# Scan layer: depthwise convolutions in a queue of their own, one per step, interleaved with the other background items

## The chip, the cores and the metric

The kernel runs on one core of one Trainium2 chip. The metric is the device time of one execution in microseconds (us); several executions are taken, and their median counts.

The core's engines run side by side and each takes its own instructions in order: TensorE (PE in the profile; PEld is its loading of weights), VectorE (DVE), ScalarE (ACT), GpSimd (POOL), and SyncE (SP), which here only issues transfers.

## The reference, cut to what matters

The program is four layers on an image batch `x` of shape (8, 64, 64, 64). Only the first one, a selective scan, is touched. For each image, with L = 64 x 64 = 4096 places, DI = 128 channels, N = 16 states and K = 4 directions (rows, columns, and both backwards):

```
xz   = layernorm(x) @ in_proj_w.T + in_proj_b          # 64 -> 2 x 128
xi,z = split(xz)
u    = silu(depthwise_conv_3x3(xi) + conv_b)           # 9 taps
for each direction k (u read in that order):
    dt, B, C = softplus(...), ..., ...                 # projections of u
    h[n,t] = h[n,t-1] * exp(dt[t] * A[n]) + dt[t] * B[n,t] * u[t]      # n = 0..15
    y     += sum_n h[n,t] * C[n,t]  + D * u
y    = layernorm(y) * silu(z)
x    = x + y @ outproj_w.T + outproj_b
```

After that come the second half of layer 0 (a small convolution block), two attention layers and a channel-mixing layer with a few steps of gradient descent.

## The kernel before, in words

`scan_layer` puts the 128 channels on the partitions. An image is worked in 16 **steps**: four directions (`k`, in the order 0, 2, 1, 3, where 1 and 3 are the column orders; for the last image 1, 3, 0, 2) by four chunks (`c`) of CH = 1024 places. A step has 16 **turns**, one for each state `n`. There are eight images (`b`), so 2048 turns, written in one long program order inside `tc.manual_schedule()`: each engine gets its instructions in the order in which the Python code issues them.

The main work of turn n, in the order of the code:

- `empty` (L692): on ScalarE, copies a finished sum of a step from PSUM into `y`.
- `spread` for turn n+1: brings B of that state on all partitions. In twelve of the sixteen turns PE does it with two bf16 products (`z`, L646). In the turns of `BY_POOL` = (0, 3, 6, 8) it is done by a broadcast transfer (`bt`, L624), a product on POOL (`product`, L636, three turns ahead) and a copy by ScalarE to PSUM (L643).
- `sum_up` (L719): PE adds the product `ct` of an earlier turn (two or three turns back, `LAG` = 2) to the sum `yps` in PSUM, as two f32 products of 512 columns with the identity. Turn 3 (`LAG + 1`) has no `sum_up`, but `begin_sum` (L710), which starts the sum of this step from `y` or from `u`; turn 7 (`LAG + 5`) has two `sum_up`.
- a slot for one **background item** (`bg.before`), see below.
- `load` (L624): a broadcast transfer of C of turn n+1 into `ct`, on SP's queue.
- `decay` (L628) for turn n+2: exp on ScalarE.
- `save_state` (L664) and `product` (L636).
- `unit`: on DVE a product (L673, not in the turns of `BY_POOL`) and the scan itself (L677); on POOL the product with C (L682).
- `bg.after`: the second half of the background item that was started one turn earlier.

The step's end feeds the next step: `hooks` issue, in fixed turns, the softplus of the next step's `dt` (L546, L549, L552) and the splitting of B into bf16 pieces (L581 to L608).

**Background items** are pairs (`make`, `use`): `make` issues the products on PE into a PSUM buffer, `use` the copy or activation that empties it, one turn later. All items of a kind take their PSUM buffer from one tag, `mm`, which has two buffers of 512 f32 columns; `z` has two of 1024, `yps` one of 1024. The class `Background` holds one queue: each turn's slot pops one item. A skipped slot leaves it alone: the slot of turn 7 always, that of turn 4 in column orders. The items are, in the order in which an image's items stand in the queue:

- for the next step, put at the front: two `lower` (PE L514 `dps`, ScalarE L522 `e`), two `step_size` (PE L532 `tps`, ScalarE L540 and L541), and in column orders first a copy of `u` in column order on ScalarE (L558, `turn`);
- `after`, for the image before: the norm of `y` (PE L296 and L309, ScalarE L300 to L316, transfers, L329 and L332, then PE L346 with DVE L350 and ScalarE L351), and the output projection of eight blocks (PE L470 and L471 `ops`, ScalarE L477, with POOL L464 for the gating product `z` times `y`, and loads `xr` and `z` on SP);
- `before`, for the image after: loads of `x` (`xn`), its norm (the same lines), the projection into the padded image `pad` (PE L383 `xps`, ScalarE L389), eight gates (PE L399 `zps`, ScalarE L406, a Silu, and a store `zd`), and eight convolutions, one per block of 512 places. A convolution is nine products on PE (L421 `vps`, one per tap) into one PSUM buffer, cut into parts; its last part is followed by a Silu on ScalarE (L430) into `u`.

Items (None, None) are spacers: they take a slot and issue nothing. A new image is entered in the queue at step 1 (`start`), the finished one at step 0. At the last step of each image `bg.drain()` issues whatever still waits; half of the next image's convolutions are then entered again (`rest`), except for the last image, all of whose convolutions are in the queue from the start.

Of the kernel before, what the change touches and what calls it, by code (L numbers as in the profile page):

```python
# [18 lines left out]
NB = 8  # L19
# [4 lines left out]
NBK = L // BK  # L24
DI = 128
N = 16
R = 4
CH = 1024
NCH = L // CH
# [136 lines left out]
class Background:  # L166
# [2 lines left out]

    def __init__(self):
        self.queue, self.last, self.late = deque(), None, []

    def add(self, items, first=False):
        if first:
            self.queue.extendleft(reversed(items))
        else:
            self.queue.extend(items)

    def later(self, do):
        self.late.append(do)

    def before(self, skip=False):
        self.now = None
        if self.queue and not skip:
            make, use = self.queue.popleft()
            self.now = (use, make() if make else None)

    def after(self):  # L190
# [7 lines left out]
    def surplus(self, turns):  # L198

        return max(0, -((turns - len(self.queue)) // (turns + 1)))  # L200

    def drain(self):
        while self.queue or self.last or self.late:
            self.before()
            self.after()


def scan_layer(cm, x_in, w, xh):

    tc, nc = cm.tc, cm.nc  # L210
    with ExitStack() as ctx:
# [156 lines left out]
        def before(b):  # L368
# [42 lines left out]
            def convolve(j):  # L411

                held = []

                def part(t0, t1):
                    def make():
                        if t0 == 0:
                            held.append(bank("vps"))
                        for t in range(t0, t1):
                            dy, dx = divmod(t, 3)  # L420
                            nc.tensor.matmul(  # L421
                                held[0].rearrange("p (r c) -> p r c", c=S), convd[:, t, :],
                                pad[:, j * rows + dy : (j + 1) * rows + dy, dx : dx + S],
                                start=(t == 0), stop=(t == 8),
                            )

                    return make

                def use(_):
                    nc.scalar.activation(u[:, bass.ts(j, BK)], held[0], AF.Silu, bias=convb)  # L430

                if b == 0:
                    return [(part(0, 5), None), (part(5, 9), use)]
                if b == NB - 1:
                    return [
                        (part(0, 3), None), (part(3, 5), None), (part(5, 7), None),
                        (part(7, 9), use),
                    ]
                return [
                    (part(0, 2), None), (part(2, 4), None), (None, None), (part(4, 6), None),  # L440
                    (part(6, 8), None), (None, None), (part(8, 9), use),
                ]

            items = [[(None, load(j)) for j in range(NBK)]]
            for blocks in (FIRST if b == 0 else (range(NBK),)):
# [4 lines left out]
        def after(b, y, zd, blocks=range(NBK)):  # L450
# [39 lines left out]
            items = norm_items(y, DI, lno, on_g, on_b, blocks)  # L490
            items.insert(-2, (None, lambda _: [load(j) for j in blocks[:3]]))
            items += [(None, begin), (None, None)]
            out = [[project_out(j), (None, None)] for j in blocks]
            return items + sum(out, [])[:-1]

        def ordered(t, k, c):

# [242 lines left out]
        def prepare(b, s):  # L740

            if b not in images:
                return None
            u, zd, y = images[b]
            k, c, i = steps(b)[s]
            dt, bc, ut, e, items, soft = project(u, k, c)
            if b == 0 and s < NCH:
                items = later.pop(s, []) + items + [(None, soft[0]), (None, soft[1])]
            bg.add(items, first=True)
            new = work.tile([DI, N], F32, name="state", tag="state", bufs=3)  # L750
            ctl = dict(
                k=k, c=c, u=u, y=y, dt=dt, bc=bc, ut=ut, dus=e, soft=soft, new=new, state=None,
                first=(i == 0), new_y=(s < NCH), turns=(s % (2 * NCH) == NCH - 1),
            )
            ctl["pieces"] = pieces(ctl)
            return ctl

        later, rest = {}, {}  # L760

        def start(b):
            u, zd, items, gates, convs = before(b)
# [6 lines left out]
                    later[s] = sum(items[s + 1 : s + 2], []) + convs[2 * s] + convs[2 * s + 1]  # L770
                later[NCH] = gates
            else:
                bg.add(gates)
                now = NBK // 2 if b < NB - 1 else NBK
                for conv in convs[:now]:
                    bg.add(conv)
                rest[b] = convs[now:]


        with tc.manual_schedule():  # L780
# [15 lines left out]
            for b in range(NB):  # L796
                for s in range(4 * NCH):
# [3 lines left out]
                    if s + 1 < 4 * NCH:  # L801
                        nxt = prepare(b, s + 1)
                    else:
                        bg.drain()
                        nxt = prepare(b + 1, 0)
                        bg.add(sum(rest.pop(b + 1, []), []))
                    hooks = {}
                    if nxt:
                        do = nxt["pieces"]
# [18 lines left out]
                    for n in range(N):  # L828
                        empty()
                        ahead(spread, n + 1)  # L830
                        if n == LAG + 1:
                            bg.before()
                            begin_sum()
                        else:
                            twice = n == LAG + 5
                            if len(pending) > LAG:
                                sum_up()
                            if twice:
                                sum_up()
                            skip = twice or (n == LAG + 2 and ctl["k"] % 2 == 1)  # L840
                            bg.before(skip and not early and not late)
                        if (n + 5) % N in BY_POOL and not (early and n + 5 == N):
                            ahead(load, n + 5, 0)
                        ahead(load, n + 1, 1)
# [1181 lines left out]
```

## Time and profile before

| what | value |
|---|---|
| time, median of 3 runs | 12565.19 us (12553.39 to 12569.26) |
| the profiled execution: its own time | 12567.77 us |
| its span, first to last instruction | 12566.0 us |
| scan layer, first to last scan | 98.2 to 7257.4 us |
| widths of images 0 to 7 | 955.2, 883.8, 880.7, 877.6, 879.3, 878.2, 903.4, 901.2 us |
| scan on DVE, L677, mean of one | 2341 ns, or 2282 ns for the first chunk of a direction |
| product with C on POOL, L682, mean of one | 2359 ns |
| product on DVE, L673, mean of one | 1215 ns |
| granted TensorE clock, mean | 0.956 |

The profile page gives the busy time of each engine over the span, a strip of 40 slices, the chain that ended last, and the costliest groups of instructions with what ended the idle time before them. The windows view gives the same busy times for any stretch; the timeline gives single instructions with, in brackets, the idle time of their engine just before them and what ended it. Widths of steps are the distance between the scans (L677) that begin them; there are 16 scans to a step. The steps of images 1 to 5 repeat each other to within a microsecond or two.

### The profile page before, as it was taken

What the parts mean: (1) busy time and instruction counts of PE and PEld (TensorE: products, weight loads), DVE (VectorE), ACT (ScalarE), POOL (GpSimd) and SP (SyncE); (2) the same over time, 40 slices, a digit from 0 to 9 for tenths busy, and PEclk for the clock granted to TensorE, in tenths of its full rate; (3) what the DMA queues carried; (4) which work ended last, traced back from release to release, by engine and by line L of the source; (5) the groups of instructions that cost most, each with busy time, mean ns of one, the idle gap of its engine ahead of it and who ended that gap; (6) DMA issues with size and microseconds to landing.
All of it is one profiled execution on the core that took longest, in us unless ns stands there. A gap on an engine that the chain in (4) does not pass through costs nothing. (4 is left out here: it accounts for less than half of the span.)

```text
span 12566.0 us, 122564 instructions
## 1 busy us (share of the span) xinstructions
PE 11561.6 (92%) x39403; PEld 4098.9 (33%) x39403; DVE 10385.0 (83%) x7362; ACT 7996.2 (64%) x10740; POOL 7424.1 (59%) x3638
## 2 busy tenths in 40 slices
PE   7899999999999999999998889999987778999999
PEld 2233233233232332332332222332324463333333
DVE  4999999999989999999899858768687685676767
ACT  4777677777776776777776536546456584555554
POOL 4999999999999999999899810000004490000000
PEclk8999999999999999999999989999998788999999
DMA  3666666666656656656566510000011110000000
GB/s 96 211 203 205 213 203 204 213 201 211 211 197 220 204 196 220 205 200 219 191 200 211 186 47 15 17 24 6 18 38 39 40 25 23 12 11 17 6 11 6
DMA packets 547044, 1562.30 MB, mean 124 GB/s; under 512 B 133040, under 2 KB 150096, under 8 KB 543824
## 3 DMA queue, kind: packets, MB, share of 16 engines
q1 hardware_dynamic: 546384, 1554.33, 37.6%
q8 instruction: 314, 5.14, 0.2%
q14 instruction: 346, 2.83, 0.1%
HBM read 1456.35 MB, written 88.87 MB: 123 GB/s over the span
## 5 line engine op out<-in xcount | busy, mean ns | idle before, releaser
L682 POOL TENSOR_TENSOR ct<-ct,h 128x1024 f32<-128x1024 f32 x2048 | 4796.0, 2359 | 456.2 <-DVE h L677 197.7
L719 PE MATMUL yps<-ct,ident 128*128 128x512 f32 x8192 | 4071.2, 626 | 4.6 <-POOL ct L682 4.6
L677 DVE TENSOR_TENSOR_SCAN h<-a,state,z 128x1024 f32<-128x1024 f32 x1536 | 3572.2, 2341 | 102.7 <-POOL ct L682 30.8
L1027 DVE TENSOR_TENSOR sum<-sum,ex 128x1024 f32<-128x1024 f32 x1920 | 2348.1, 1223 | 617.9 <-ACT ex L1020 481.2
L1020 ACT ACTIVATE ex<-sc 128x1024 f32<-128x1024 f32 x2048 | 1967.9, 1024 | 1359.8 <-PE sc L1015 1359.8
L628 ACT ACTIVATE a<-dt,amat 128x1024 f32<-128x1024 f32 x2048 | 2344.7, 1146 | 611.5 <-DVE h L677 606.9
L673 DVE TENSOR_TENSOR z<-z,e 128x1024 f32<-128x1024 f32 x1536 | 1866.5, 1215 | 391.1 <-PE z L646 240.2
L719 PEld LDWEIGHTS yps<-ct,ident 128*128 128x128 f32 x8192 | 1444.8, 192 | 2033.2 <-issue 1816.6
L1034 PE MATMUL av<-ex,v 128*64 128x512 f32 x8192 | 1950.0, 604 | 0.0
L1015 PE MATMUL sc<-q,k 16*128 16x512 f32 (+1 forms) x8192 | 1562.2, 623 | 4.2 <-ACT q L1008 3.1
L677 DVE TENSOR_TENSOR_SCAN h<-a,z 128x1024 f32<-128x1024 f32 x512 | 1162.7, 2282 | 101.6 <-ACT z L643 85.9
L646 PE MATMUL z<-bs,pick 48*128 48x512 bf16 x3072 | 941.6, 387 | 324.7 <-DVE h L677 290.0
L636 POOL TENSOR_TENSOR bt<-bt,e 128x1024 f32<-128x1024 f32 x512 | 1209.1, 2362 | 4.7 <-DMA bt<-bc 4.7
L1341 POOL TENSOR_TENSOR gt<-gt,pad 128x1024 f32<-128x1024 f32 x16 | 34.9, 2179 | 1572.0 <-ACT gt L1340 1492.7
L1034 PEld LDWEIGHTS av<-ex,v 128*64 128x64 f32 x8192 | 512.2, 136 | 1332.8 <-issue 1278.9
L1015 PEld LDWEIGHTS sc<-q,k 16*128 16x128 f32 (+1 forms) x8192 | 528.4, 184 | 1016.2 <-issue 977.3
L643 ACT COPY z<-bt 128x1024 f32<-128x1024 f32 x512 | 519.4, 1014 | 460.4 <-DVE h L677 237.7
L646 PEld LDWEIGHTS <-pick 48*128 48x128 bf16 x3072 | 180.1, 95 | 1592.7 <-issue 756.6
L421 PE MATMUL vps<-pad,convd 128*128 128x512 f32 x1152 | 540.6, 594 | 0.0
L1714 DVE RECIPROCAL r<-e 128x512 f32<-128x512 f32 x128 | 420.7, 3324 | 0.0
L1717 POOL TENSOR_TENSOR r<-r,half 128x512 f32<-128x512 f32 x128 | 162.6, 1270 | 361.6 <-issue 188.8
L664 ACT COPY state<-h 128x1 f32<-128x1 f32 x2048 | 359.4, 176 | 1.6 <-DVE h L677 1.6
(408 smaller groups left out, 10581.9 us busy)
## 6 DMA issues: line engine op xcount, KB each, us to landing
ct<-bc SPq DMA_DIRECT2D x2048, 512.0 KB
bt<-bc SPq DMA_DIRECT2D x512, 512.0 KB
x<-x SPq DMA_DIRECT2D x12, 2048.0 KB
bc<-e SPq DMA_DIRECT2D x256, 64.0 KB
zd<-z SPq DMA_DIRECT2D x64, 256.0 KB
z<-zd SPq DMA_DIRECT2D x64, 256.0 KB
x<-x SPq DMA_DIRECT2D x32, 512.0 KB
part<-x SPq DMA_DIRECT2D x128, 128.0 KB
```

The lines of the kernel that those rows point to most:

```text
L421: nc.tensor.matmul(held[0].rearrange("p (r c) -> p r c", c=S), convd[:, t, :], pad[:, j * rows + dy : (j + 1) * rows + dy, dx : dx + S], s ...
L628: ctl["exp", n] = nc.scalar.activation(ctl["a", n], ctl["dt"], AF.Exp, scale=amat[:, ctl["k"], n : n + 1])
L636: nc.gpsimd.tensor_tensor(bt, bt, ctl["dus"], ALU.mult)
L646: nc.tensor.matmul(z[:, bass.ts(i, BK)], pick[:, n : n + 1].to_broadcast([3 * N, DI]), ctl["bs"][:, bass.ts(i, BK)], start=True, stop=True,)
L673: first = nc.vector.tensor_tensor(z, z, ctl["dus"], ALU.mult)
L677: nc.vector.tensor_tensor_scan(h[:, flip], a[:, flip], z[:, flip], 0.0 if state is None else state[:, n : n + 1], ALU.mult, ALU.add,)
L682: freed[at] = nc.gpsimd.tensor_tensor(ct, ct, h, ALU.mult)
L719: nc.tensor.matmul(ctl["ps"][:, bass.ts(i, BK)], cm.ident, ct[:, bass.ts(i, BK)], start=False, stop=(n == N - 1 and not ctl["turns"]),)
L1015: nc.tensor.matmul(sc[:, e, :], k[r : r + d, bass.ts(j, 128)], qs[i][r : r + d, :], start=True, stop=True,)
L1020: nc.scalar.activation(ex, sc, AF.Exp)
L1027: nc.vector.tensor_tensor(sums[i], sums[i], ex, ALU.add)
L1034: nc.tensor.matmul(avs[i][r, :], v[:, j, r], ex[:, e, :], start=(j == 0), stop=(j == TQ - 1))
```

## The change

The convolutions get a queue of their own (`groups`), one group of parts for each convolution. A group is opened only when all its parts fit in the slots that are left in the current step, and when nothing that was put at the front for the next step still waits. While a group is open, its parts alternate with items of the ordinary queue (`item` says that the last slot went to one), unless as many parts are left as slots. `credit` allows one group per step, two in the steps of image 6. The groups become available when the image's last projection has been issued. `finish` issues what is still missing when a step is about to read `u`; it takes the place of the drain at the last step of an image. In column orders the skipped slots are those of turns 3 and 7, except in the first step of the second direction of the pair, which skips turn 7 alone. The spacers inside a convolution and between the output projections go; each gate is followed by two spacers instead.

```diff
 class Background:
     def __init__(self):
         self.queue, self.last, self.late = deque(), None, []
+        self.groups, self.open, self.done = deque(), deque(), {}
+        self.first = self.credit = 0
+        self.item = False
     def add(self, items, first=False):
         if first:
             self.queue.extendleft(reversed(items))
+            self.first += len(items)
...
-    def before(self, skip=False):
+    def before(self, skip=False, slots=0):
         self.now = None
-        if self.queue and not skip:
-            make, use = self.queue.popleft()
+        if skip:
+            return
+        src = None
+        if self.open:
+            if not self.first and (self.item or len(self.open) >= slots or not self.queue):
+                src = self.open
+        elif self.groups and self.credit and not self.first and slots >= len(self.groups[0]):
+            src = self.open = self.groups.popleft()
+            self.credit -= 1
+        if src is None and self.queue:
+            src = self.queue
+            self.first = max(0, self.first - 1)
+        self.item = src is not self.open
+        if src:
+            make, use = src.popleft()
             self.now = (use, make() if make else None)
...
+    def finish(self, b, count):
+        while self.done.get(b, NBK) < count:
+            self.credit = 1
+            self.before(slots=NBK)
+            self.after()
...
                 def use(_):
                     nc.scalar.activation(u[:, bass.ts(j, BK)], held[0], AF.Silu, bias=convb)
-                if b == 0:
-                    return [(part(0, 5), None), (part(5, 9), use)]
-                if b == NB - 1:
-                    return [
-                        (part(0, 3), None), (part(3, 5), None), (part(5, 7), None),
-                        (part(7, 9), use),
-                    ]
-                return [
-                    (part(0, 2), None), (part(2, 4), None), (None, None), (part(4, 6), None),
-                    (part(6, 8), None), (None, None), (part(8, 9), use),
-                ]
+                    if b:
+                        bg.done[b] += 1
+                cuts = (0, 5, 9) if b == 0 else (0, 3, 5, 7, 9) if b == NB - 1 else (0, 2, 4, 6, 8, 9)
+                parts = [(part(t0, t1), None) for t0, t1 in zip(cuts, cuts[1:])]
+                return parts[:-1] + [(parts[-1][0], use)]
...
-            out = [[project_out(j), (None, None)] for j in blocks]
-            return items + sum(out, [])[:-1]
+            return items + [project_out(j) for j in blocks]
...
             k, c, i = steps(b)[s]
+            bg.finish(b, 2 * c + 2 if s < NCH and k == 0 else NBK)
...
             else:
-                bg.add(gates)
-                now = NBK // 2 if b < NB - 1 else NBK
-                for conv in convs[:now]:
-                    bg.add(conv)
-                rest[b] = convs[now:]
+                bg.done[b] = 0
+                bg.add([(None, lambda _: bg.groups.extend(deque(conv) for conv in convs))])
+                for gate in gates:
+                    bg.add([gate, (None, None), (None, None)])
...
                     else:
-                        bg.drain()
                         nxt = prepare(b + 1, 0)
-                        bg.add(sum(rest.pop(b + 1, []), []))
+                    bg.credit = 2 if b == NB - 2 else 1
+                    columns = ctl["k"] % 2 == 1 and s % (2 * NCH) != NCH
+                    idle = () if early or late else (LAG + 1, LAG + 5) if columns else (LAG + 5,)
...
+                        slots = 0 if early or late else sum(m not in idle for m in range(n, N))
                         if n == LAG + 1:
-                            bg.before()
+                            bg.before(n in idle, slots)
                             begin_sum()
                         else:
-                            twice = n == LAG + 5
                             if len(pending) > LAG:
                                 sum_up()
-                            if twice:
+                            if n == LAG + 5:
                                 sum_up()
-                            skip = twice or (n == LAG + 2 and ctl["k"] % 2 == 1)
-                            bg.before(skip and not early and not late)
+                            bg.before(n in idle, slots)
```

More of the change, by code (lines that the diff above doesn't have):

```diff
@@ L200, in surplus @@
         return max(0, -((turns - len(self.queue)) // (turns + 1)))
+    def finish(self, b, count):
[3 more added lines that the diff above has]
+            self.after()
     def drain(self):
-        while self.queue or self.last or self.late:
+        while self.queue or self.open or self.last or self.late:
             self.before()
@@ L756, in prepare @@
             return ctl
-        later, rest = {}, {}
+        later = {}
         def start(b):
```

## The prediction

> **Notation.** Step s (0 to 15) is one of an image's 16 (direction, chunk) pairs, turn n (0 to 15) one state inside it; images are 0 to 7. Turn lengths are read in the timeline as the distance between two scans (L677).
>
> **What bounds the kernel now.** I read the page's first part, then the table of windows cut at image and step borders, then the timeline of the turns that were long.
>
> ```profile
> PE 11561.6 (92%) x39403; PEld 4098.9 (33%) x39403; DVE 10385.0 (83%) x7362; ACT 7996.2 (64%) x10740; POOL 7424.1 (59%) x3638
> ```
>
> These are means over four layers; only the first, from 98.2 to 7257.4 us, is touched. The windows of images 0, 3 and 6, then of steps 3, 12 and 14 of image 3 (columns: PE, PEld, DVE, ACT, POOL busy, clock, DMA share, GB/s):
>
> ```profile
> 98.20:1053.36 955.16, 859.11 (x1914) 284.58 (x1915) 821.25 (x464) 663.73 (x940) 826.25 (x383) 0.95 0.57 188
> 2817.78:3695.35 877.57, 833.77 (x1897) 273.21 (x1896) 822.02 (x467) 637.59 (x923) 839.46 (x393) 0.98 0.63 208
> 5452.81:6356.18 903.37, 857.73 (x1945) 282.22 (x1943) 822.75 (x467) 648.28 (x932) 839.04 (x393) 0.98 0.61 202
> ...
> 2982.05:3033.90 51.85, 46.78 (x110) 14.83 (x108) 51.42 (x32) 36.37 (x54) 51.85 (x25) 1.00 0.64 215
> ...
> 3467.90:3527.07 59.17, 53.20 (x118) 18.40 (x117) 50.63 (x29) 45.32 (x61) 48.85 (x23) 0.91 0.61 200
> ...
> 3582.99:3638.53 55.54, 53.53 (x124) 18.91 (x123) 51.00 (x30) 38.48 (x54) 52.24 (x25) 0.97 0.56 197
> ```
>
> POOL is the wall. Step 3 is POOL from end to end (51.85 of 51.85). Image 3 keeps POOL busy 839.46 of 877.57 us, so 38 us are idle; DVE, at 822, is just behind. POOL's floor for a plain step is (839.46 - 8 x 1.26 of gating products, L464) / 16 = 51.8 us; DVE's is 12 turns of 3.50 and 4 of 2.26, 51.0 us. What can be won is POOL's idle time, and it lies where convolutions and gates are: step 12 idles 59.17 - 48.85 = 10.3 us. Two causes show in the timeline.
>
> (a) The run of eight gates. ScalarE, POOL and DVE around the start of step 12:
>
> ```profile
> 3464.90 1.28 ACT L406 ACT_TABLE_LOAD   x1
> 3466.20 0.69 ACT L406 ACTIVATE z<-zps,inb 128x512 f32<-128x512 f32 x1
> 3466.78 1.02 ACT L643 COPY z<-bt 128x1024 f32<-128x1024 f32 x1
> 3467.82 1.28 ACT L628 ACT_TABLE_LOAD   x1
> ```
> ```profile
> 3474.22 2.35 POOL L682 TENSOR_TENSOR ct<-ct,h 128x1024 f32<-128x1024 f32 x1 [1.54 <-DVE h L677]
> 3480.59 2.35 POOL L682 TENSOR_TENSOR ct<-ct,h 128x1024 f32<-128x1024 f32 x1 [4.02 <-DVE h L677]
> ```
>
> Each Silu between two Exp costs 1.28 + 0.69 + 1.28 = 3.25 us of ScalarE. One per turn, beside 1.15 (L628) and 0.17 (L664), is over 4.5 us against a 3.50 turn, so decays and copies come late, DVE stops and POOL starves. Turns 15, 0, 1, 2 there last 6.2, 3.8, 6.4, 4.2 us against 2.3, 3.4, 3.4, 2.2: 9.3 us lost.
>
> (b) A convolution that stays open over a step border. PE, then DVE in step 14; PE in step 10, where none is open:
>
> ```profile
> 3595.38 1.12 PE L532 MATMUL tps<-ut,wst 128*128 128x512 f32 x2 [2.01 <-ACT e L522]
> 3596.35 3.59 PE L710 MATMUL yps<-y,ident 128*128 128x512 f32 x4
> 3599.87 0.60 PE L646 MATMUL z<-bs,pick 48*128 48x512 bf16 x2
> ```
> ```profile
> 3600.61 1.23 DVE L673 TENSOR_TENSOR z<-z,e 128x1024 f32<-128x1024 f32 x1 [2.54 <-PE z L646]
> ```
> ```profile
> 3369.17 1.13 PE L532 MATMUL tps<-ut,wst 128*128 128x512 f32 x2
> ```
>
> The open convolution holds one of two "mm" PSUM buffers, so both dps and the first tps share the other: tps waits for the copy of the second dps (L522), and behind it in PE's queue stand the start of the sum (L710) and z of turn 5, for which DVE waits. Turn 4 lasts 6.4 us instead of 3.5; in step 10 it lasts 3.7.
>
> **What the Trainium skill says.** "ScalarE: Activation LUTs", What ACT_TABLE_LOAD costs: about 1283 ns a load, and a drain of about 1380 ns with it. The trace agrees on the load (1.28) and not on a further drain: the ACTIVATE starts 1.30 after its load. "PSUM — Partial Sum Buffer", Specifications: 8 banks of 512 FP32 values a partition. mm has 2 buffers of 512, z 2 of 1024, yps 1 of 1024: 2 + 4 + 2 = 8, so no third mm buffer stands by; the 2.01 above agrees. "Perfetto Trace Analysis", Identifying the Most-Contended Engine: occupancy serves for the other engines, matmul busy time does not; I therefore count PE by issue intervals, 0.855 us a 512-column f32 product and 0.53 for a pair of z.
>
> **The change, part by part,** along the program order of both kernels. No product, activation or transfer of the layer is removed or added: the parts change places. What goes is the drain at each image's last step, where all waiting items were issued at once.
>
> 1. A convolution now starts only if it ends in the same step, one per step, in steps 10 to 15 of the image before and 0 and 1. Before, they fill steps 12 to 15, 0 and 1 with 11, 11, 13, 14, 14 and 9 taps. The wait of (b) goes in steps 13, 14, 15, 0: turn 4 drops from 6.5, 6.4, 5.0, 7.8 towards 3.5. The drain at step 15 goes too: its turn 0, 5.2, becomes 3.5. Next in line is PE around turns 6 and 7: two taps and then two sums, 3.95 + 3.42 = 7.4 us against 3.48 + 2.26 on DVE. Step 14 has that today: its turn 8 lasts 4.69, 1.2 over. That stays: 51.0 + 1.2 + 0.5 for a Silu moved behind turn 0 = 52.7.
> 2. Gates come every third slot at most, so (a) goes. A step then has up to three Silu, 9.8 us on top of some 38 of ScalarE: under 51. But in steps 11 and 13 a convolution's and a gate's Silu stand beside the column copy (L558, 2.0 us) at the step's head: 6.5 us where step 14 shows 2.8 idle. The sum's start and z of turn 5 queue behind; I take 1.8 us each.
> 3. Column steps skip turn 3 instead of 4, which moves tps behind the sum's start (L710) and z. A gain in order; I book nothing beyond 1.
> 4. The norm of y alternates with convolutions in steps 0 and 1: 77 PE instructions each (76 and 75 before), 38.8 + 15 x 0.855 = 51.6 us, close to the wall. Booked at 53.5 and 53.0.
> 5. The output projections lose their spacer. All eight gating products fall into step 4: POOL 51.8 + 10.1 = 61.9; seven scalings of y (L350, 0.6 each) fall into step 3: DVE 51.0 + 4.2 = 55.2; eight of xn into step 8: 50.1 + 4.8 = 54.9. On SP the loads of xr and z, the stores of x, zd and xn's loads keep their number and move past the ct and bt loads (L624); covered by POOL's backlog of ct, which step 4 has.
>
> Images 1 to 5, in order of steps 10 to 15, 0, 1: before 53.7 + 55.6 + 59.2 + 55.9 + 55.5 + 56.8 + 58.6 + 53.9 = 449.2; after 52.7 + 54.5 + 52.0 + 54.5 + 52.7 + 53.7 + 53.5 + 53.0 = 426.6. Steps 2 to 9: before 428.4; after 52 + 55.2 + 61.9 + 52 + 52 + 52 + 54.9 + 51.9 = 431.9. Net -19.1 each, -95.5 for five.
> Image 0: steps 10 to 15 before 328.9, after 320.1: -8.8.
> Image 6: steps 0 to 11 as above without 12 to 15: -4.5. Steps 12 to 15 hold all eight convolutions of image 7 today, 63.7 + 60.8 + 62.8 + 66.7 = 253.9. After: 52.5, 54.0, then two in step 14, eight parts in a row at 4.17 a turn, 57.5. Two are still missing at step 15, and all 18 taps are issued at once: today 13 make turn 0 17.4 us (13.9 over), so 18 cost 13.9 + 5 x 0.855 = 18.2, 69.2. Sum 233.2: -20.7.
> Image 7: only its eight output projections move: 0.
>
> Sum -129.5 on the profiled execution's 12567.8 us (span 12566.0 and 1.8 around it); the median of the runs is 2.6 lower: **12436**.
>
> **Unknown costs.** Two Silu at a step's head: nothing, if ScalarE's idle time absorbs them, to 2.9 us, the stall of today. Residue at turn 8: nothing (POOL's lag covers it, and 51.8 is the floor) to 1.5. Projections in every turn: from -2 us an image (DVE work lies beside POOL's) to 2.8 us each, the mean of PE's ten measured waits for z of L464 (27.7 us).
>
> **The rivals.**
> - POOL alone decides: all residues lie behind its backlog, eight steps at 51.8 = 414.7, so -34.5 + 3.5 an image: -155, with images 0 and 6 -205 in all: 12360. For it: step 3 shows such a step; against: turn 8 of step 14. Chance 0.13.
> - ScalarE takes the place of the bank: Silu at the head delays the sum's start in four column steps by 2.9, so 11.6 of the 19.1 come back: -37, -20 in images 0 and 6: 12508. For: ScalarE is in order and L710 needs L692; against: ScalarE has 17 us idle in step 14. Chance 0.13.
> - Slower: in step 4 each output projection on PE waits for a product (L464) that POOL was given one turn before instead of two; behind it in PE's queue stand z and the sums, behind those SP's ct loads. If all 56 in the seven images that meet this wait 2.8 us with POOL idle: +157 - 129.5 = +27, 12593. It decides from 2.3 us each. Against: POOL has two ct and a product, 6 us, to do meanwhile. Chance 0.08.
> - The change not doing what it says: true only at the border to image 7, where 18 taps come in a lump; in the sum.
>
> **Numbers.** Forecast 0.66, own range 12400 to 12480. The range to 12360 and 12515 takes half of the first rival and most of the second. A measurement here tells 0.2% (25 us) from no change. Faster 0.86, same 0.06, slower 0.08.
>
> **What would show it.** Right: no wait of tps on L522 in steps 13 to 15; turn 4 at 3.5 to 4; turns 15 to 2 about step 12 at their floor; POOL idle 15 to 25 us an image; image 3 near 858 us; turn 0 of image 6, step 15, near 21 us. Wrong: POOL idle in step 4, turn 4 of steps 11 and 13 above 6 us, or steps 0 and 1 above 55.

## The result and the profile after

The changed kernel takes 12587.76 us (median of 16 runs, 12576.96 to 12615.21), the kernel before, run beside it, 12568.98 us. The ratio is 1.0017 (95% interval 1.0009 to 1.0025): 19 us **slower**, where 12436 had been forecast. The profiled execution has a span of 12581.3 us at a granted clock of 0.951 (0.956 before). Widths, waits and clocks below are each of one profiled execution; that of e2 lies 19 us above the median of its runs and that of e5c 17. The scan layer is 16.5 us longer, of which 14.8 lie in image 7; the other three layers are equal to a microsecond or two.

In the kernel after, the lines of `before` stand 26 further down (the convolution is L447, its Silu L456, the gate's Silu L432) and those from L464 on 19 or 20: dps L533 and its copy L541, tps L551 with L559 and L560, the loads and products `z` L665, `product` L655, `z` on DVE L692, scan L696, product with C L701, copy of y L711, start of the sum L729, `sum_up` L738, gating product L484, projection L490 and L491.

The page's first part after:

```profile
PE 11602.1 (92%) x39403; PEld 4122.0 (33%) x39403; DVE 10387.3 (83%) x7362; ACT 8007.8 (64%) x10745; POOL 7425.3 (59%) x3638
```

Counts and work are those of before (ScalarE has five instructions more); PE is busy 40.5 us longer with the same 39,403 instructions. (An f32 product of 512 columns stands as two instructions in these traces: the start of a sum, two products in the code, is `x4`.) The windows view of the kernel after, cut as before: images 0, 3 and 6, then steps 3, 12 and 14 of image 3.

```profile
98.38:1056.11 957.73, 871.32 (x1926) 289.11 (x1926) 821.50 (x464) 668.23 (x944) 826.46 (x383) 0.94 0.57 188
...
2815.06:3694.50 879.44, 841.61 (x1896) 275.40 (x1896) 822.25 (x467) 639.61 (x924) 839.11 (x393) 0.97 0.63 207
...
5459.32:6358.07 898.75, 858.15 (x1932) 282.77 (x1932) 823.25 (x467) 642.62 (x928) 838.48 (x393) 0.98 0.61 203
...
2980.37:3036.86 56.49, 55.00 (x115) 17.30 (x116) 55.57 (x37) 37.44 (x56) 52.40 (x25) 0.91 0.65 209
...
3474.93:3525.36 50.43, 49.82 (x119) 17.61 (x118) 49.87 (x29) 39.07 (x56) 50.43 (x25) 1.00 0.69 224
...
3585.28:3638.71 53.43, 52.44 (x122) 18.04 (x120) 51.01 (x29) 40.30 (x56) 52.07 (x25) 1.00 0.64 209
```

Image 3 takes 879.44 us, 1.9 more than before, with POOL busy 839.11: its idle time is 40 us where it was 38. Step 12, which idled 10.3 us for the gates, now has POOL busy from end to end, 50.43 of 50.43. So what was to go there went; as much has come elsewhere. Mean widths of the steps of images 1 to 5 (distance between the scans that begin them):

| step | 0 | 1 | 2 | 3 | 4 | 5 | 6 | 7 | 8 | 9 | 10 | 11 | 12 | 13 | 14 | 15 | image |
|---|---|---|---|---|---|---|---|---|---|---|---|---|---|---|---|---|---|
| before | 58.5 | 53.9 | 51.8 | 51.8 | 54.3 | 58.2 | 53.6 | 52.9 | 51.9 | 55.8 | 53.7 | 55.9 | 59.4 | 55.7 | 55.7 | 56.8 | 879.9 |
| after | 56.1 | 55.4 | 53.3 | 56.4 | 61.0 | 51.6 | 51.8 | 52.5 | 56.5 | 53.6 | 55.2 | 57.4 | 50.5 | 58.7 | 54.9 | 55.8 | 880.6 |
| e3, below | 51.9 | 55.1 | 55.0 | 57.2 | 60.3 | 51.6 | 51.8 | 52.5 | 54.8 | 52.0 | 53.6 | 52.9 | 51.0 | 53.4 | 53.6 | 54.2 | 860.9 |

Steps 12, 0, 5, 6 and 9 are shorter after; 3, 4 and 8 longer, as part 5 had booked; steps 1, 2, 10 and 11 are 1.5 longer and step 13 is 3.0 longer, where part 1 had booked a gain for steps 10, 11 and 13. The waits from 100 to 7200 us (waiting engine and line, what it waited for, us in all, times, longest) say what has grown. Before:

```profile
DVE z L673 <- PE z L646: 236.0, 207, 6.5
POOL ct L682 <- DMA ct<-bc: 172.0, 167, 4.5
ACT dt L540 <- PE tps L532: 17.4, 19, 2.2
```

After:

```profile
DVE z L692 <- PE z L665: 269.1, 239, 6.6
POOL ct L701 <- DMA ct<-bc: 209.1, 207, 5.1
ACT dt L559 <- PE tps L551: 118.0, 102, 5.2
PE yps L729 <- ACT y L711: 72.6, 52, 4.6
```

ScalarE's wait for tps rises from 17 to 118 us. PE's wait for the copy of y ahead of the sum's start, 72.6 us after, is 5.7 us before. And POOL, the wall, waits 37 us more for its own operand C; its wait for the scan (DVE `h`) goes the other way, from 182.7 to 137.5. What has gone is the wait of tps for the copy of dps: 49.8 us on PE before, and not among the 60 longest groups after.

One place shows them together: PE in the kernel after, image 2, step 14, turns 3 to 6.

```profile
2712.83 0.60 PE L665 MATMUL z<-bs,pick 48*128 48x512 bf16 x2
2714.31 3.68 PE L729 MATMUL yps<-y,ident 128*128 128x512 f32 x4 [0.87 <-ACT y L711]
2717.92 1.03 PE L665 MATMUL z<-bs,pick 48*128 48x512 bf16 x2
2718.88 3.78 PE L738 MATMUL yps<-ct,ident 128*128 128x512 f32 x4
2722.45 1.24 PE L551 MATMUL tps<-ut,wst 128*128 128x512 f32 x2
2723.53 1.88 PE L738 MATMUL yps<-ct,ident 128*128 128x512 f32 x4
2725.25 1.02 PE L551 MATMUL tps<-ut,wst 128*128 128x512 f32 x2
2726.21 0.60 PE L665 MATMUL z<-bs,pick 48*128 48x512 bf16 x2
```

PE reaches the start of the sum (L729), waits 0.87 us for the copy of y, and only then, between z of turn 5 (2717.92) and z of turn 7 (2726.21), come both tps. DVE and POOL pay for it:

```profile
2727.01 1.23 DVE L692 TENSOR_TENSOR z<-z,e 128x1024 f32<-128x1024 f32 x1 [2.07 <-ACT dt L559]
```
```profile
2726.61 2.37 POOL L701 TENSOR_TENSOR ct<-ct,h 128x1024 f32<-128x1024 f32 x1 [1.33 <-DMA ct<-bc]
```

DVE's releaser here is named as ScalarE's L559; the product it needs, z of turn 7, starts on PE at 2726.21, directly ahead of DVE's 2727.01.

The order isn't all that happens here. The windows view of the same stretch, with the granted clock as the third number from the end:

```profile
2716.07:2722.89 6.82, 6.82 (x10) 2.29 (x9) 6.18 (x5) 3.00 (x5) 6.82 (x3) 0.50 0.08 32
2722.89:2726.21 3.32, 3.32 (x9) 1.15 (x7) 2.05 (x1) 2.38 (x4) 2.39 (x2) 1.00 0.56 178
```

From 2716.07 on TensorE runs at half its clock, for 6.8 us: z takes 1.03 us instead of 0.60, and the four instructions of a sum 3.78 instead of the 1.88 that they take just after. In these traces the clock is recorded as full or half, in stretches of 3.4 us or a multiple. Images 1 to 5 spend 47.8 us each at half clock after, 35.5 before.

The longest waits for the copy of y are in steps 11 and 13, 3.7 and 4.6 us on average. In these steps a convolution's and a gate's Silu both stand in turns 0 and 1 on ScalarE, ahead of that copy. PE in image 3, step 13:

```profile
3535.19 0.60 PE L665 MATMUL z<-bs,pick 48*128 48x512 bf16 x2 [0.50 <-DVE h L696]
3540.39 3.78 PE L729 MATMUL yps<-y,ident 128*128 128x512 f32 x4 [4.60 <-ACT y L711]
3544.11 1.03 PE L665 MATMUL z<-bs,pick 48*128 48x512 bf16 x2
```

In steps 11 and 13 of all five images the clock falls to half in this wait or with the sum's start behind it.

In image 2, step 14, turn 6 lasts 5.66 us (3.48 before), turn 8 5.34 (4.69 before), and turn 4, where the stall of the PSUM bank was, 4.18 (6.38 before): 2.2 won, 2.8 lost. Over images 1 to 5 turn 6 of the seven column steps that skip turn 3 (8 to 15 without 12) averages 4.49 us; before, it takes 3.42 to 3.69 in these. Where turns 3 to 8 see no half clock, it is 3.42 to 3.75, and 4.55 in step 15: much of the 4.49 is clock.

### The profile page after: what moved, and what is told of

It is laid out like the page before. It is cut to its first block, busy times and chain, and to the rows that moved or that the text cites. A ratio compares the mean times of both kernels' runs of the same rounds, so it can differ in the third digit from the quotient of the medians.

```text
span 12581.3 us, 122514 instructions
## 1 busy us (share of the span) xinstructions
PE 11602.1 (92%) x39403; PEld 4122.0 (33%) x39403; DVE 10387.3 (83%) x7362; ACT 8007.8 (64%) x10745; POOL 7425.3 (59%) x3638
## 5 line engine op out<-in xcount | busy, mean ns | idle before, releaser
L701 POOL TENSOR_TENSOR ct<-ct,h 128x1024 f32<-128x1024 f32 x2048 | 4797.5, 2359 | 471.6 <-DMA ct<-bc 211.1
L738 PE MATMUL yps<-ct,ident 128*128 128x512 f32 x8192 | 4111.5, 631 | 0.0
L696 DVE TENSOR_TENSOR_SCAN h<-a,state,z 128x1024 f32<-128x1024 f32 x1536 | 3571.0, 2341 | 101.6 <-ACT z L662 49.7
L692 DVE TENSOR_TENSOR z<-z,e 128x1024 f32<-128x1024 f32 x1536 | 1866.2, 1215 | 430.6 <-PE z L665 276.1
L738 PEld LDWEIGHTS yps<-ct,ident 128*128 128x128 f32 x8192 | 1455.8, 194 | 2039.5 <-issue 1818.7
L665 PE MATMUL z<-bs,pick 48*128 48x512 bf16 x3072 | 952.3, 391 | 346.0 <-DVE h L696 300.0
L696 DVE TENSOR_TENSOR_SCAN h<-a,z 128x1024 f32<-128x1024 f32 x512 | 1162.0, 2281 | 71.8 <-ACT z L662 52.4
L655 POOL TENSOR_TENSOR bt<-bt,e 128x1024 f32<-128x1024 f32 x512 | 1208.4, 2360 | 4.8 <-DMA bt<-bc 4.8
L665 PEld LDWEIGHTS <-pick 48*128 48x128 bf16 x3072 | 181.2, 95 | 1615.9 <-issue 787.6
L447 PE MATMUL vps<-pad,convd 128*128 128x512 f32 x1152 | 541.5, 594 | 0.0
```

Of the source, the lines that this page charges most:

```text
L447: nc.tensor.matmul(held[0].rearrange("p (r c) -> p r c", c=S), convd[:, t, :], pad[:, j * rows + dy : (j + 1) * rows + dy, dx : dx + S], s ...
L655: nc.gpsimd.tensor_tensor(bt, bt, ctl["dus"], ALU.mult)
L665: nc.tensor.matmul(z[:, bass.ts(i, BK)], pick[:, n : n + 1].to_broadcast([3 * N, DI]), ctl["bs"][:, bass.ts(i, BK)], start=True, stop=True,)
L692: first = nc.vector.tensor_tensor(z, z, ctl["dus"], ALU.mult)
L696: nc.vector.tensor_tensor_scan(h[:, flip], a[:, flip], z[:, flip], 0.0 if state is None else state[:, n : n + 1], ALU.mult, ALU.add,)
L701: freed[at] = nc.gpsimd.tensor_tensor(ct, ct, h, ALU.mult)
```

## The experiments

**Theory A**, formed on this trace: the move of tps behind the start of the sum costs the time. Before, the first tps runs while PE would wait for the copy of y anyway; behind the sum's start it is paid in full, z of turn 7 and the sums come late, the buffers of C come free late, their transfers start late, and POOL waits for them.

Its rivals: **theory B**, ScalarE's Silu at the head of column steps, and **theory C**, the output projections without spacers ate the gain. A further cause, tried in e2, is groups that open before turn 8 and put taps beside the double sum of turn 7. Other rivals stand with the runs they belong to.

In the kernel before, in image 3, step 10, PE has no wait left between the first tps and the sum's start:

```profile
3369.17 1.13 PE L532 MATMUL tps<-ut,wst 128*128 128x512 f32 x2
3370.13 3.59 PE L710 MATMUL yps<-y,ident 128*128 128x512 f32 x4
3373.65 0.60 PE L646 MATMUL z<-bs,pick 48*128 48x512 bf16 x2
```

### e1_idle_old: the skipped slot of before

```diff
-idle = () if early or late else (LAG + 1, LAG + 5) if columns else (LAG + 5,)
+idle = () if early or late else (LAG + 2, LAG + 5) if ctl["k"] % 2 else (LAG + 5,)
```

> The changed kernel with the skipped slots of column steps as before (turns 4 and 7 instead of 3 and 7), so that the first tps stands ahead of the sum's start again. Theory A (PE's queue in turns 3 to 8: tps used to run while PE waited for ScalarE's copy of y, behind the sum's start it is paid in full and makes z, the sums and through them the C transfers late): turn 6 of column steps falls from a mean of 4.5 and 4.3 us (steps 8 to 11 and 12 to 15 of images 1 to 6) to 3.5 to 3.7, image widths fall by 5 to 9 us, 12520 to 12550 in all. Theory B (ScalarE's Silu at the head of column steps): no change, 12580 to 12595. Theory C (output projections in every turn): no change.

Measured: 12494.57 us, ratio 0.9944 (0.9931 to 0.9958). The images 1 to 5 average 870.2 us, 10.4 less than after. Steps 0 to 7 keep their sum (437.8, after 438.1) and steps 8 to 15, the column steps, go from 442.6 to 432.4. Turn 6 of the seven is back at 3.42 to 3.69. POOL's wait for C falls from 209.1 to 153.4 us, PE's for the copy of y from 72.6 to 11.7. That is more than theory A had expected (5 to 9 us an image, 12520 at best).

In step 11 of image 3 the sum's start begins 14.3 us after the step's first scan in both kernels. The tps of e1 stands in a wait that PE has anyway, here PE in the kernel after, then in e1:

```profile
3428.03 0.60 PE L665 MATMUL z<-bs,pick 48*128 48x512 bf16 x2
3432.30 3.68 PE L729 MATMUL yps<-y,ident 128*128 128x512 f32 x4 [3.66 <-ACT y L711]
```
```profile
3400.40 0.60 PE L665 MATMUL z<-bs,pick 48*128 48x512 bf16 x2
3402.87 1.13 PE L551 MATMUL tps<-ut,wst 128*128 128x512 f32 x2 [1.87 <-ACT e L541]
3404.70 3.78 PE L729 MATMUL yps<-y,ident 128*128 128x512 f32 x4 [0.70 <-ACT y L711]
```

The edit also gives step 12 back the skipped slot that it had before, so that items from there on move by a slot: the two Silu at a step's head leave step 13 (5.6 us shorter) for step 14 (1.1 longer). Steps 8 to 11 are the clean test, since both kernels issue the same items in them, and only the place of tps differs: 222.6 us after, 217.0 here. So theory A holds for 5.6 us of the 10.4, and theory C can't be the main cause. The 4.5 us of steps 12 to 15 are tps and Silu together, and theory B isn't refuted there. Less time at half clock (28.6 us an image instead of 47.8) is part of both.

### e2_late_open and e3_old_late: groups opened only from turn 8

```diff
-slots = 0 if early or late else sum(m not in idle for m in range(n, N))
+slots = 0 if early or late or n <= LAG + 5 else sum(m not in idle for m in range(n, N))
```

e2 has this edit alone, e3 this and that of e1.

> The changed kernel with a convolution group opened from turn 8 on only; turns 4 to 6 keep ordinary items. Theory A: turn 8 of the eight steps with a convolution falls from 5.3 to 4.2 to 4.5 us, about 1 us a step, 7 us an image, about 12535. Theories B and C: no change beyond 5 us in all; B even slower where the Silu stays at the head of the next step.

> Both edits of the two runs before at once. Theory A: the two add, 12 to 16 us an image, 12460 to 12500. Theories B and C: 12580 to 12595.

Measured: e2 12547.47 us, 0.9989 (0.9982 to 0.9995), images 1 to 5 at 875.8; e3 12444.46 us, **0.9901 (0.9886 to 0.9916)**, images 1 to 5 at 860.9. By images 1 to 5 the edits win 4.8 and 10.4 us an image alone and 19.7 together, more than theory A's 12 to 16; by the ratios 0.0028 and 0.0073 alone and 0.0116 together, so that a gain beyond their sum is not clear of noise. e3 beats both kernels. Its image 3, and the same turns of image 2, step 14, on PE:

```profile
2771.75:3635.99 864.24, 833.34 (x1896) 273.42 (x1896) 821.93 (x468) 635.93 (x922) 838.67 (x392) 0.99 0.62 211
```
```profile
2674.87 0.60 PE L665 MATMUL z<-bs,pick 48*128 48x512 bf16 x2
2675.41 1.12 PE L551 MATMUL tps<-ut,wst 128*128 128x512 f32 x2
2676.80 3.68 PE L729 MATMUL yps<-y,ident 128*128 128x512 f32 x4 [0.27 <-ACT y L711]
2680.42 0.60 PE L665 MATMUL z<-bs,pick 48*128 48x512 bf16 x2
2680.95 3.70 PE L738 MATMUL yps<-ct,ident 128*128 128x512 f32 x8
2684.49 1.02 PE L551 MATMUL tps<-ut,wst 128*128 128x512 f32 x2
2685.44 0.60 PE L665 MATMUL z<-bs,pick 48*128 48x512 bf16 x2
```

The first tps (2675.41) stands ahead of the sum's start and fills the wait for y, of which 0.27 is left. From z of turn 5 to z of turn 7 it is 5.0 us against 8.3 after: one tps of some 1.0 less, and some 2.2 from the clock, which is full here (z 0.60 against 1.03, the eight instructions of two sums 3.70 against 3.78 and 1.88).

The edit of e2 does more than clear turn 7. It moves the convolutions' Silu too: in e2 and e3 no step has the two Silu in its turns 0 and 1, and steps 11 and 14, which had them in e1, are 3.1 and 2.4 us shorter in e3. Averages over images 1 to 5, in us an image (the wait is PE's for the copy of y directly ahead of the sum's start, in steps 8 to 15; in e1 and e3 a tps fills part of it):

| | before | after | e1 | e2 | e3 | e5c, below |
|---|---|---|---|---|---|---|
| width of an image | 879.9 | 880.6 | 870.2 | 875.8 | 860.9 | 881.3 |
| wait ahead of the sum's start | 0.1 | 10.8 | 1.1 | 4.6 | 1.0 | 3.1 |
| time at half clock | 35.5 | 47.8 | 28.6 | 49.8 | 16.4 | 41.0 |

The kernels with little of both are the fast ones. What the half clock costs by itself was not tested: no run changes it alone. POOL's wait for C in e3, over the same 100 to 7200 us:

```profile
POOL ct L701 <- DMA ct<-bc: 93.0, 119, 5.1
```

209.1 us after, 153.4 in e1, 93.0 here: the chain from PE's queue to the transfers of C has moved. Part of the wait only changed its name: POOL's wait for the scan rises from 137.5 to 204.5. That the transfers start late because `sum_up` frees their buffers late is read from the code and these lines; it isn't shown by a run. A sixth buffer for C would have tested it alone and wasn't tried.

### e4_spaced: the spacers between output projections restored

```diff
-return items + [project_out(j) for j in blocks]
+out = [[project_out(j), (None, None)] for j in blocks]
+return items + sum(out, [])[:-1]
```

> The changed kernel with the spacers between the output projections restored. Theory C: steps 3 to 5 of images 1 to 5, 56.5 + 60.4 + 51.8 now, fall by 3 us or more in sum, 12560 or less. Theory A: step 4 falls to 55 and step 5 rises to 58, sum unchanged; the later items shift by 7 slots, so image 6 has 27 taps in a lump at its last step instead of 18, 8 us more: 12590 to 12600.

Measured: 12583.44 us, 1.0023 (1.0015 to 1.0030); images 1 to 5 at 878.6. Step 4 shrinks from 61.0 to 57.3, and steps 2 and 5 grow by 4.9 and 3.1. Steps 3 to 5, which theory C had falling by 3 us or more, take 168.7 us against 169.0. Theory C falls. Images 1 to 5 are 2 us narrower each, image 6, with its larger lump of taps, is 14.6 wider, and nothing is left in the time.

### e5c_b_skip3: the move alone, on the kernel before

```diff
-bg.before()
+bg.before(ctl["k"] % 2 == 1 and not early and not late)
...
-skip = twice or (n == LAG + 2 and ctl["k"] % 2 == 1)
+skip = twice
```

> The kernel before with one part of the change alone: column steps skip the slot of turn 3 instead of that of turn 4, so that both tps stand behind the start of the sum (L710). Theory A: slower than before by 4 to 8 us an image in columns (turn 6 at 4 to 5 us where it is 3.5 now), 30 to 60 us in all. My prediction's step 3 (nothing, or a gain where a convolution is open, since tps no longer blocks L710 and z): 12500 to 12568.

Measured: 12593.22 us, 1.0019 (1.0012 to 1.0025). In the whole time it costs by itself as much as the whole change does, but not where theory A said: images 1 to 5 average 881.3, 1.4 us more than before, where 4 to 8 had been expected. Images 0, 6 and 7 are 13.5, 7.4 and 12.6 us longer in this trace; why these is open. Inside images 1 to 5 it is mixed: steps 13 and 14 win 1.6 and 1.7 us (turn 4 of them falls from 6.5 and 6.3 to 4.1 and 3.8), where a convolution is open and tps would wait for the bank; steps 9 and 10, in which none is open, lose 2.1 and 2.0, step 15 loses 1.7. PE's wait for the copy of y, 0.1 us an image before, is 0.5 to 0.6 us in each of steps 9 to 11 and 13 to 15. So the move is a remedy for stall (b). In the changed kernel, in which no group straddles a border, there is nothing left to remedy and the price remains.

### e6c_skip7 and e9_late_skip7: no skipped slot but turn 7

```diff
-idle = () if early or late else (LAG + 1, LAG + 5) if columns else (LAG + 5,)
+idle = () if early or late else (LAG + 5,)
```

e6c makes this edit on the kernel after; e9 makes it on e3.

> The changed kernel with the slot of turn 7 alone skipped in all steps, so that in columns tps stand at turns 3 and 4 (3 and 5 in e1_idle_old, 4 and 5 in the changed kernel). If what counts is the first tps ahead of the sum's start (theory A), about as fast as e1_idle_old, 12480 to 12520, with turn 6 at 3.5. If what counts is that two background items do not follow each other in turns 3 to 5 (rival D), as slow as the changed kernel, 12570 to 12600.

Measured: 12569.79 us, 0.9996 (0.9988 to 1.0005), images 1 to 5 at 882.1. Not what theory A had expected (12480 to 12520, turn 6 at 3.5; it is 4.7): the time is at the edge of its rival's 12570 to 12600, for which two items in a row are the cost. It isn't clean either: with tps done at turn 4 groups can open a turn earlier, and every later item moves up by one slot in each column step. e9 takes the first of these away.

> From e3 (groups opened only from turn 8, the skip of before); here the skip of turn 4 goes too, so that column steps issue their two tps at turns 3 and 4 and everything after them one turn earlier; since groups open from turn 8 in both, no convolution can start sooner than in e3, which is what blurred e6c. Theory A, narrow (what costs is the first tps behind the start of the sum; the second is behind it in every variant): images 1 to 5 stay at 859 to 865 us as in e3, ratio to before 0.989 to 0.992. Rival (PE's queue in turns 3 to 6 needs the free slot itself: begin_sum, four sum products and two tps in a row leave z(5) late whichever tps goes first): turn 4 or 5 of steps 10 to 15 lengthens by 1 us or more, images 1 to 5 at 867 to 872, ratio 0.995 to 0.998.

Measured: 12490.01 us, 0.9945 (0.9928 to 0.9961), images 1 to 5 at 867.3, as the rival said (the ratio lies between the two), but not where it said. Steps 10 to 15 take 320.9 us against 318.8 in e3, and turn 4 of them 25.6 against 27.7 in all, so two tps at turns 3 and 4 cost turn 4 nothing. The 6.4 us above e3 are a balance: beside the 2.1 of steps 10 to 15, steps 0 to 3 win 5.5, steps 4 to 7 lose 7.4, and steps 8 and 9 lose 2.4. The loss in step 4 can be read. PE, then DVE and POOL in e9, image 2, step 4:

```profile
2160.41 1.97 PE L491 MATMUL ops<-z,wout 128*64 128x512 f32 x2 [2.78 <-POOL z L484]
2162.30 5.80 PE L738 MATMUL yps<-ct,ident 128*128 128x512 f32 x8
2168.04 0.60 PE L665 MATMUL z<-bs,pick 48*128 48x512 bf16 x2
```
```profile
2168.85 1.23 DVE L692 TENSOR_TENSOR z<-z,e 128x1024 f32<-128x1024 f32 x1 [7.39 <-PE z L665]
```
```profile
2170.36 2.36 POOL L701 TENSOR_TENSOR ct<-ct,h 128x1024 f32<-128x1024 f32 x1 [2.95 <-DMA ct<-bc]
```

The projection waits 2.78 us for its gating product, z and the sums queue behind it, in part at half clock (eight instructions in 5.80 us, 3.70 in e3), DVE stands 7.39 us, the transfers of C come late and POOL itself stands 2.95: turn 8 lasts 10.95 us. The wait is the one that the slower rival of the prediction names, met in a kernel where the projections have moved by a slot or more. In the kernel after, step 4 has POOL busy nearly throughout (60.02 of 60.40 us in image 3), and it isn't met. What of e6c's loss is groups opened earlier and what is this shift stays open.

### e7c_gates_run: e3 with its gates in a run again

```diff
-bg.add([gate, (None, None), (None, None)])
+bg.add([gate])
```

> e3_old_late with the spacers behind the gates taken out, so that eight Silu of gates come in successive turns again. If part (a) of the prediction is right, images 1 to 5 are 7 to 10 us wider than in e3_old_late (about 869), in the steps 9 to 11 that hold the gates. If the spacing was worth nothing (rival), 860 to 863. Image 6 differs besides (no lump of taps), so only images 1 to 5 are read.

Measured: 12520.91 us, 0.9958 (0.9942 to 0.9975), images 1 to 5 at 870.9. Steps 10 and 11 grow from 53.6 and 52.9 to 59.0 and 56.3, turns 1, 2 and 4 of step 10 to 4.9, 4.2 and 5.7. The spacing of the gates is worth 10.0 us an image; 9.3 had been read off turns 15 to 2 of the kernel before.

### e8c_straddle: e3 with convolutions that cross the border of a step

```diff
-elif self.groups and self.credit and not self.first and slots >= len(self.groups[0]):
+elif self.groups and self.credit and not self.first and (0 < slots <= 4 or slots == 99):
...
-            self.before(slots=NBK)
+            self.before(slots=99)
```

> e3_old_late with each convolution started with at most four slots left, so that its fifth part comes after the step border and its PSUM buffer is held across it. If part (b) is right, tps at turn 3 waits for L541 and turn 4 of steps 10 to 15 is 6.3 to 6.6 us instead of 4.5 to 5.1, images 1 to 5 are 10 to 16 us wider than in e3_old_late. If the held buffer costs nothing (rival), 858 to 864.

Measured: 12618.18 us, 1.0037 (1.0024 to 1.0049), images 1 to 5 at 891.9: **31 us an image**, two to three times what was expected. PE, then DVE, in image 2, step 14:

```profile
2747.45 1.59 PE L551 MATMUL tps<-ut,wst 128*128 128x512 f32 x2 [2.01 <-ACT e L541]
```
```profile
2753.13 1.23 DVE L692 TENSOR_TENSOR z<-z,e 128x1024 f32<-128x1024 f32 x1 [3.38 <-PE z L665]
```

It is stall (b) again, the same 2.01 us for the same copy as before the change, and turn 4 of steps 10, 11, 13 and 14 lasts 6.8 to 6.9 us. Turn 4 of steps 15 and 0 takes 8.5 and 8.2. Steps 10 to 15 are 18.8 us longer than in e3, steps 0 and 1 9.3, steps 4 and 7 6.2. Images 1 to 5 spend 43.7 us each at half clock, 16.4 in e3. How much of the 31 us this is, and why it is so much more than the stalls of the kernel before, which has the same wait in fewer steps, was not taken apart further.

### e10_image6: fewer taps in the lump ahead of image 7

```diff
-bg.add([gate, (None, None), (None, None)])
+bg.add([gate, (None, None)] + ([(None, None)] if b < NB - 1 else []))
...
-bg.credit = 2 if b == NB - 2 else 1
+bg.credit = 2 if b == NB - 2 and s > 9 else 1
```

> From e3: one spacer fewer behind each gate of the last image, and the second group per step only from step 10 of image 6, so that fewer convolutions are left for the lump before step 15's first turn (9 taps in place of 18). Lump theory (PE's 0.855 us per tap with nothing beside it): turn 0 of step 15 falls from 19 us by about 8, steps 14 and 15 together by 8 less what more taps cost in step 14, image 6 about 8 us narrower than in e3 (888), time about 12436, ratio 0.9895 where e3 has 0.9901. Rival (PE is full in steps 12 to 15 of image 6, and a tap costs its 0.855 us wherever it stands): image 6 within 2 us of e3, the same ratio as e3.

Measured: 12440.62 us, 0.9905 (0.9889 to 0.9922); image 6 takes 882.8 us, e3 887.8. Turn 0 of step 15 falls from 20.86 to 13.13 us: 7.7, near the 8 expected, for 20 taps that became 11. Steps 12 to 14 give 4.4 of it back and steps 10 and 11 two more: 1.3 us remain of the edit, and the rival, for which a tap costs its time wherever it stands, comes closer than the forecast of 8. The rest of the 5 us lies in steps 3 and 4, before the edit acts. In the time of the whole kernel the 5 us can't be seen: within the intervals it is e3.

## Why the prediction was wrong

**The step that failed is part 3**: "Column steps skip turn 3 instead of 4 ... A gain in order; I book nothing beyond 1." It saw the item that moves and not what it had been hidden in. The sentence names what tps is moved behind, the sum's start and z, and doesn't ask what PE does in turn 3 without it: wait for the copy of y, 0.87 us in step 14 and 4.60 in step 13. Undone in e1, the move gives 5.6 us an image in steps 8 to 11, where nothing else differs, and with what it does to steps 12 to 15 10.4 in each of images 1 to 5; the ratio falls by 0.0073, some 92 us. On the kernel before (e5c) the same move costs only 1.4 us in these images, because there it also removes stall (b).

**The second is the residue at turn 8**, a term of part 1. It was booked at 1.2 us for a turn of 4.69, "Step 14 has that today". Measured, turn 8 lasts 5.33 to 5.41 us in seven steps of an image, 1.9 over, and behind late sums there is no slack to take it up. With groups opened from turn 8 on it is 3.4 to 4.2 in steps 10 to 15 and 0 of e3. Alone that edit is worth 4.8 us an image, with part 3 mended 9.3; as it moves the Silu too, this is the price of the residue and of the next term together.

**The third is a term of part 2**, the two Silu at a step's head, booked at 1.8 us: they keep PE 3.7 and 4.6 us from the sum's start in steps 11 and 13, and turn 4 lasts 5.7 and 6.0 us there (3.7 and 6.5 before). Beneath all three lies a price taken as fixed: 0.855 us a product of 512 columns. Where the clock falls to half the two products of a sum take 3.78 us instead of 1.88, and no term asked whether the new order would bring more of that.

From the kernel after to e3 the ratio falls by 0.0116, or 146 us of the 152 that the forecast was off.

Point by point:

- **Part 1, stall (b) goes**: right. PE's wait of tps for the copy of dps is down to 0.6 us in all (49.8 before), turn 4 of steps 14 and 15 is 4.0 and 4.1 (6.3 and 5.0 before), and e8c gives the price of bringing it back. In steps 11 and 13 the Silu took the bank's place: turn 4 rose to 5.7 in the one and only fell from 6.5 to 6.0 in the other.
- **Part 2, stall (a) goes**: right, by step 12 at its floor and by e7c. The double Silu at a step's head, booked at 1.8 us, is under-sized: in e1, which puts it into steps 11 and 14, these take 56.0 us where steps 10, 12, 13 and 15 take 52.2 to 54.1, so 2 to 4.
- **Part 4, steps 0 and 1**: booked 53.5 and 53.0, measured 56.1 and 55.4, in e3 51.9 and 55.1. The sum of the two was right once the groups open late; step 1 is PE from end to end in e3.
- **Part 5, the projections**: booked 55.2, 61.9 and 54.9 for steps 3, 4 and 8, measured 56.4, 61.0 and 56.5. Right to 1.6 us; e4 wins little by undoing it.
- **Image 6**: turn 0 of step 15 was put near 21 us and lasts 19.14, for 18 taps at 0.87. Steps 12 to 15 take 235.6 us, forecast 233.2.
- **Image 7**: booked at 0, measured 14.8 longer, 7.3 of it in steps 0 to 7, its column steps, and 7.5 in steps 13 to 15, which skip no slot. It spends 146.8 us at half clock, 104.4 before. e1 takes 17.0 us back, 9.9 of them in steps 13 to 15, where it issues what the kernel after does; so this part isn't shown to be the move.
- **The sum**: for images 1 to 5 the parts promised -19.1 us each and after brought +0.7. e3 brings -19.0. That this agrees to 0.1 is luck: single steps of e3 lie up to 3.0 off what was booked (step 2 at 55.0 for 52), and turn 4 of steps 10 to 15 without 12 is 4.4 to 5.2, not 3.5. What it does show is that the gain of parts 1 and 2 was there to be had.
- **The rivals**: the time lies within 6 us of the slower rival's 12593, but for another reason; its own mechanism was met only in e9. The second rival, ScalarE in the bank's place, had a true mechanism in two of its four steps, 11 and 13. No rival held that a moved item could cost in column steps. What the prediction said would show it wrong did come, with turn 4 of step 13 at 6.0 and steps 0 and 1 above 55.

## What to carry to other kernels

An item in an in-order queue costs what its engine would have done without it: ask what the engine waits for at the old place before moving the item, and book the item's whole length at the new one if that wait had covered it. An item that holds one of two shared accumulation buffers should not be open while another kind needs both; but once that is arranged, a detour that was made for the same stall is only a cost, so test such remedies one by one. When an instruction takes twice its time in a trace without a wait in front of it, look at the granted clock of that stretch before naming a cause. And when an edit moves one item of a queue, list what else moves by a slot with it: read the effect from the steps in which nothing else does.

## What the runs showed of the hardware

The start of the sum reads `y` through PE either in row or in column order. In the kernel after, by groups of lines and by shape, in steps 4 to 7 (rows) and then in steps 8 to 15 (columns) of image 3:

```profile
L729 PE MATMUL yps<-y,ident 128*128 128x512 f32 x12 | 5.6, 592 | 0.0
```
```profile
L729 PE MATMUL yps<-y,ident 128*128 128x512 f32 x28 | 25.9, 1057 | 10.8 <-ACT y L711 10.8
```

The same instruction takes 592 ns in row order and 1057 ns in column order, where its moving operand is read with a stride (1033 in the kernel before). The four of a step's start then take 3.68 us (image 2, step 14) instead of 1.88 (image 3, step 5, in rows). At half clock the two orders meet: over the scan layer of the kernel after, an instruction of this line that reads `y` takes on average 592 ns in rows at full clock and 1060 at half, and 1058 and 1060 in columns. So here the strided read, and not the clock, sets the pace in columns. It fits that turns 3 to 6 are tight on PE in column steps; no run takes the stride away. The prediction had priced every f32 product of 512 columns alike, though its own line of the column start shows 3.59 us for two.
